# A graph layer on one core: where the adjacency and two pairs of h are turned

## Chip, cores, metric

One Trainium2 chip, one core. The metric is the device time of one execution in microseconds (us), the median of several; lower is better. A profile is one further execution taken by the hardware profiler; its span differs from the timed median by a few us.

TensorE does the matmuls, VectorE and ScalarE the elementwise work. Transfers (DMA) are issued by SyncE, ScalarE and GpSimd, each its own in program order (its queue). A semaphore is a counter that engines wait on; each transfer here has one that tells of its landing. The clock is the share of full speed that the profile's records grant to TensorE; it is 1.00 or one half.

## The reference

```python
h = jnp.maximum(layernorm(x), 0.0)                 # x: (64, 256, 256)
out = x + gnn(h, adj, ...)                         # adj: (64, 256, 256), 0/1

def gnn(x, mask, ...):
    h = relu(bn(conv1d(x^T, conv1_w)))             # 1 tap
    h = bn(conv1d(h, conv2_w, pad=8))              # 17 taps
    x_conv = relu(h + x^T)^T
    s = x @ w_se.T + b_se                          # 3 numbers a node
    A = exp(-dist(s, s)) * mask
    x_nmp = A @ relu(x @ w_msg.T + b_msg)
    # a GRU cell: gates r, z, n from [x_conv, x_nmp] and x
    return (1 - z) * n + z * x
```

All is float32. The 64 graphs are handled in 32 pairs; four pairs are a batch, so there are eight batches, 0 to 7.

## The kernel before

The convolution of 17 taps is done in the frequency domain: VectorE transforms a batch forward, TensorE multiplies 16 bins by filter weights (`products`, two bins a call), VectorE transforms back. Then come the gates of the four pairs, during which the next batch is prepared. The weights are streamed for each batch into nine buffers, three bins ahead of their use:

```python
def load_kind(b, n, kind):
    b, n = b + n // BINS, n % BINS
    if b < NB and (n < BINS - 1 or kind < 2):
        WB[b, n, kind] = work.tile([P, DC, D], FP, name="wb", bufs=9)
        ...
        nc.sync.dma_start(out=WB[b, n, kind], in_=filt[m][:, ...])
```

TensorE needs h with channels on the partitions. A pair's h is either transposed on TensorE (`transpose_h`) or by a DMA transpose of its 16-bit halves, in three steps: turn, sort, join. adj is turned in the same way, kept in DRAM and loaded again when it is needed:

```python
def turn_h(i):
    t = late.tile([P, 2 * MC, W], U16, name="hh").bitcast(FP)
    ...                                   # ScalarE: relu(x * rstd + shift) into hh
    TURNED[i] = late.tile([P, 2 * MC, W], U16, name="halves")
    nc.sync.dma_start_transpose(out=TURNED[i]..., in_=t...)
    load_x(i + 2)

def sort_h(i):
    HH[i] = late.tile([P, 2 * MC, W], U16, name="hh")
    ...                                   # four nc.sync.dma_start, HH <- TURNED

def join_h(i):
    ...                                   # two nc.scalar.copy, HT <- HH

def turn_adj(i):
    HALVES[i] = late.tile([P, 2 * MC, W], U16, name="halves")
    nc.sync.dma_start_transpose(out=HALVES[i], in_=adj[...].bitcast(U16))

def keep_adj(i):
    ADJD[i] = dram.tile([...], U16, name="halves_d", bufs=6)
    for k in range(2 * MC):
        nc.sync.dma_start(out=v[k], in_=HALVES[i][:, k])
```

`halves` has one buffer, shared by turned h and turned adj, and all these transfers and the weights go through SyncE's queue, in program order. The end of a batch (`i`: its first pair, `nxt` = i + 4):

```python
gates(i + 2, 0, wait, ...)                # wait() holds turn_h(nxt + 4)
sort_h(nxt + 4)
turn_adj(nxt);     keep_adj(nxt)
aggregate(i + 3);  finish(i + 1);  load_adj(nxt)
turn_adj(nxt + 1); keep_adj(nxt + 1)
gates(i + 2, 1)
join_adj(nxt)
turn_adj(nxt + 2); keep_adj(nxt + 2)
turn_adj(nxt + 3); keep_adj(nxt + 3)
...                                       # then the next batch's products
```

## Time and profile before

Before: 1912.29 us, the median of 4 runs (1909.44 to 1914.62). From the trace I read two lengths for each batch: "products", from the start of the first to the end of the last matmul that reads `wb`, and "gates", from there to the next batch's first (in batch 7, to TensorE's end).

| batch | 0 | 1 | 2 | 3 | 4 | 5 | 6 | 7 |
|---|---|---|---|---|---|---|---|---|
| products, us | 62.2 | 65.8 | 64.7 | 61.0 | 61.6 | 61.0 | 61.4 | 52.7 |
| gates, us | 168.4 | 164.2 | 164.2 | 164.2 | 164.2 | 164.2 | 164.2 | 153.2 |

Batch 7 has the same products as the others and nothing to prepare behind it. How the profile is read: the page gives each engine's busy time, forty slices of the span and the costliest groups. The waits name the engine and line that waited, what released it, then the total in us, how often, and the longest. The queue in order of time gives start, duration, engine and line of the issue, and what is moved where.

ScalarE waits too:

```profile
ACT adj L423 <- DMA adjh<-halves_d: 77.2, 8, 12.2
...
ACT hT L645 <- DMA hh<-halves: 9.4, 1, 9.4
```

The first is the joining of adj that has just been kept by that chain, the second the joining of the sixth pair's h in batch 0.

### The profile page before, as it was taken

What the parts mean: (1) busy time and instruction counts of PE and PEld (TensorE: products, weight loads), DVE (VectorE), ACT (ScalarE), POOL (GpSimd) and SP (SyncE); (2) the same over time, 40 slices, a digit from 0 to 9 for tenths busy, and PEclk for the clock granted to TensorE, in tenths of its full rate; (3) what the DMA queues carried; (4) which work ended last, traced back from release to release, by engine and by line L of the source; (5) the groups of instructions that cost most, each with busy time, mean ns of one, the idle gap of its engine ahead of it and who ended that gap; (6) DMA issues with size and microseconds to landing.
All of it is one profiled execution on the core that took longest, in us unless ns stands there. A gap on an engine that the chain in (4) does not pass through costs nothing.

```text
span 1915.2 us, 21916 instructions
## 1 busy us (share of the span) xinstructions
PE 1822.1 (95%) x7486; PEld 1133.5 (59%) x7486; DVE 1366.1 (71%) x2591; ACT 731.1 (38%) x1447; POOL 226.1 (12%) x368
## 2 busy tenths in 40 slices
PE   6898999799998999899998999989999899999997
PEld 4686444774557645595446844486455855478453
DVE  5877669496786958688495966959677784979522
ACT  3424542255322643236422554225532364224321
POOL 3210101101011010110111110110011100011000
PEclk9988999899998999999999999999999999999999
DMA  6868335662357433583246633575345833445011
GB/s 189 264 215 212 88 68 121 199 180 56 87 122 225 133 86 75 148 253 84 55 104 181 195 76 67 127 213 164 67 87 121 256 103 70 103 140 147 0 42 36
DMA packets 252896, 247.00 MB, mean 129 GB/s; under 512 B 145410, under 2 KB 179486, under 8 KB 252785
## 3 DMA queue, kind: packets, MB, share of 16 engines
q1 hardware_dynamic: 218741, 183.24, 34.7%
q0 software_dynamic: 31936, 60.48, 13.5%
q10 hardware_dynamic: 2108, 1.89, 0.3%
q8 instruction: 59, 0.97, 0.2%
q14 instruction: 52, 0.43, 0.1%
HBM read 156.54 MB, written 44.30 MB: 105 GB/s over the span
## 4 chain that ended last, share of the span: by engine, by line
PE 69%; DMA 14%; SPq 2%; DVE 2%; ACT 1%; issue 0%; POOLq 0%; POOL 0%; ACTq 0%; DVEq 0%
PE acc L480 59%; PE aux L480 7%; DMA halves<-in_adj_dram 5%; DMA halves_d<-halves 5%; DMA wb<-filt 2%; PE aux L484 2%; SPq L403 1%; PE aux L803 1%; DMA halves<-hh 1%; DMA hh<-halves 1%; ACT hh L622 0%; SPq L636 0%; ACT e L804 0%; DVE Yv L59 0%; DVE T L65 0%
## 5 line engine op out<-in xcount | busy, mean ns | idle before, releaser
L480 PE MATMUL acc<-xnm,w_ih 128*128 128x512 f32 x768 | 353.2, 593 | 0.0
L480 PE MATMUL acc<-hT,w_hh 128*128 128x512 f32 x768 | 350.5, 593 | 0.0
L480 PE MATMUL acc<-Yv,w_ih 128*128 128x512 f32 x768 | 342.7, 596 | 1.1 <-ACT Yv L763 1.1
L480 PEld LDWEIGHTS acc<-Yv,w_ih 128*128 128x128 f32 x768 | 146.0, 191 | 184.3 <-issue 180.8
L480 PEld LDWEIGHTS acc<-xnm,w_ih 128*128 128x128 f32 x768 | 145.0, 190 | 175.7 <-issue 175.5
L480 PEld LDWEIGHTS acc<-hT,w_hh 128*128 128x128 f32 x768 | 144.2, 190 | 164.3 <-issue 155.2
L865 DVE SCALAR_TENSOR_TENSOR gn<-tr,gn 128x512 f32<-128x512 f32 x64 | 44.2, 690 | 211.5 <-ACT tr L863 211.2
L863 ACT ACTIVATE tr<-acc,b_rz 128x512 f32<-128x512 f32 x64 | 44.0, 687 | 326.0 <-PE acc L480 326.0
L480 PE MATMUL acc<-V,wb 128*128 128x128 f32 x1024 | 133.6, 287 | 0.0
L891 POOL DMA_DIRECT2D out_dram<-y x64 | 39.4, 620 | 790.7 <-DVE y L890 789.3
L480 PE MATMUL acc<-U,wb 128*128 128x128 f32 x1024 | 125.3, 277 | 6.8 <-DMA wb<-filt 6.8
L480 PEld LDWEIGHTS acc<-V,wb 128*128 128x128 f32 x1024 | 128.6, 204 | 0.0
L480 PEld LDWEIGHTS acc<-U,wb 128*128 128x128 f32 x1024 | 121.2, 194 | 10.5 <-DMA wb<-filt 7.0
L480 PE MATMUL acc<-hT,w_c 128*128 128x512 f32 x256 | 118.3, 605 | 3.9 <-ACT hT L645 2.0
L59 DVE SCALAR_TENSOR_TENSOR V<-T,V 128x256 f32<-128x256 f32 (+2 forms) x224 | 121.6, 610 | 0.3
L480 PE MATMUL acc<-Sv,wb 128*128 128x128 f32 x512 | 74.5, 292 | 44.2 <-DMA wb<-filt 44.2
L745 DVE TENSOR_TENSOR Yv<-p,acc 128x512 f32<-128x512 f32 x32 | 21.9, 686 | 130.6 <-PE acc L480 95.5
L480 PE MATMUL aux<-e,msg 128*128 128x256 f32 x464 | 104.9, 379 | 0.0
L423 ACT COPY adj<-adjh 128x1024 uint16<-128x1024 uint16 x58 | 73.9, 1345 | 77.2 <-DMA adjh<-halves_d 77.2
L480 PEld LDWEIGHTS aux<-e,msg 128*128 128x128 f32 x464 | 87.3, 190 | 17.5 <-issue 7.2
L480 PEld LDWEIGHTS acc<-Sv,wb 128*128 128x128 f32 x512 | 67.7, 205 | 48.5 <-DMA wb<-filt 45.3
L736 ACT COPY p<-acc 128x512 f32<-128x512 f32 x56 | 32.8, 586 | 160.7 <-PE acc L480 132.2
(153 smaller groups left out, 2772.2 us busy)
## 6 DMA issues: line engine op xcount, KB each, us to landing
wb<-filt SPq DMA_DIRECT2D x376, 256.0 KB
y<-in_x_dram POOLq DMA_DIRECT2D x64, 256.0 KB, 5.6
out_dram<-y POOLq DMA_DIRECT2D x64, 256.0 KB, 5.6
x<-in_x_dram SPq DMA_DIRECT2D x60, 256.0 KB
halves_d<-halves SPq DMA_DIRECT2D x116, 128.0 KB
adjh<-halves_d POOLq DMA_DIRECT2D x116, 128.0 KB, 6.1
hh<-halves SPq DMA_DIRECT2D x112, 128.0 KB
filt<-fo POOLq DMA_DIRECT2D x20, 252.0 KB, 5.6
```

Source lines behind the costliest of these rows:

```text
L59: return self.step(out, lambda: self.v.scalar_tensor_tensor(out, x, s, y, op0=ALU.mult, op1=ALU.add))
L403: nc.sync.dma_start(out=v[k], in_=HALVES[i][:, k])
L423: nc.scalar.copy(v[:, j], u[:, j])
L480: nc.tensor.matmul(p, w, v, **kw)
L484: nc.tensor.transpose(p, v, ident)
L736: nc.scalar.copy(p1, p[0])
L745: nc.vector.tensor_sub(re, pv[0], pv[2])
L803: nc.tensor.matmul(p[:, :N], ZT[rows_q, :P], ZT[rows_q, P:], start=True, stop=True)
L863: nc.scalar.activation(tr, pr, AF.Tanh, bias=b_rz[:, dc:dc + 1], scale=0.5)
L865: nc.vector.scalar_tensor_tensor(gn, tr, 1.0, gn, op0=ALU.add, op1=ALU.mult)
L891: nc.gpsimd.dma_start(out=rows(out, G * i + g), in_=row_tile(Y[i], g))
```

## The change

The intent: spread the turnings of adj over the gates' stretch, one behind each sorting of h, so that one instead of four stands in front of the next batch's weights; and in batch 0, turn the fifth pair's h on TensorE, without the queue, and the sixth pair's h earlier.

```diff
-            if i >= PB:
+            if i > PB:                       # shift is only needed by turn_h
...
-        run(norm_steps(nxt if b == 0 else nxt + 1)[0])
+        if b == 0:
+            norm(nxt)
+        else:
+            run(norm_steps(nxt + 1)[0])
...
         if b == 0:
-            turn_h(nxt)
+            pace.add(norm_steps(nxt + 1)[0], normed[1])
...
             transpose_a(i + 1)
-            sort_h(nxt)
+            transpose_h(nxt)
...
         message(i + 2)
-        if b > 0:
-            turn_h(nxt + 1)
+        pace.flush(normed[1])
+        turn_h(nxt + 1)
 
         def wait():
             pace.flush(scaled)
-            if b == 0:
-                join_h(nxt)
...
         load_adj(i + 3)
-        if b == 0:
-            pace.flush(normed[1])
-            turn_h(nxt + 1)
         sort_h(nxt + 1)
+        turn_adj(nxt)
+        keep_adj(nxt)
...
         sort_h(nxt + 2)
+        turn_adj(nxt + 1)
+        keep_adj(nxt + 1)
...
         sort_h(nxt + 3)
+        turn_adj(nxt + 2)
+        keep_adj(nxt + 2)
...
         sort_h(nxt + 4)
-        turn_adj(nxt)
-        keep_adj(nxt)
+        turn_adj(nxt + 3)
+        keep_adj(nxt + 3)
...                                           # the other three are gone from here
```

More of the change, by code (lines that the diff above doesn't have):

```diff
@@ L1008 @@
         join(0)
-        if b == 0:
-            pace.add(norm_steps(nxt + 1)[0], normed[1])
         pace.add(norm_steps(nxt + 2)[0], normed[2])
@@ L1036 @@
         load_adj(i + 3)
-        if b == 0:
-            pace.flush(normed[1])
-            turn_h(nxt + 1)
         sort_h(nxt + 1)
+        turn_adj(nxt)
+        keep_adj(nxt)
         def early():
@@ L1084 @@
         load_adj(nxt)
-        turn_adj(nxt + 1)
-        keep_adj(nxt + 1)
         gates(i + 2, 1)
         join_adj(nxt)
-        turn_adj(nxt + 2)
-        keep_adj(nxt + 2)
-        turn_adj(nxt + 3)
-        keep_adj(nxt + 3)
         pace.flush(joined[3])
```

## The prediction

> **What bounds the kernel now.** I read the busy table and the slices first, then TensorE's waits, then the DMA queue (SyncE) in order of time, then windows of 20 us.
>
> ```profile
> PE 1822.1 (95%) x7486; PEld 1133.5 (59%) x7486; DVE 1366.1 (71%) x2591; ACT 731.1 (38%) x1447; POOL 226.1 (12%) x368
> ...
> PEclk9988999899998999999999999999999999999999
> ```
> TensorE is busy 95% of the span, VectorE, the next, 71%. So the kernel is bound by TensorE, and only what TensorE waits for, or runs slowly through, can be won. The clock row shows a dip at four slices beyond the start: something stops TensorE there.
>
> TensorE's waits, in total, times, longest:
> ```profile
> PE acc L480 <- DMA wb<-filt: 50.9, 7, 10.2
> ...
> PE acc L480 <- ACT hT L645: 2.0, 1, 2.0
> ```
> Seven waits for `wb`, the filter weights of the products in the frequency domain, are more than half of TensorE's 93 us of idleness. Asked window by window, one (6.8 us) lies at 161 us, inside the first batch's products; the other six (10.2, 9.3, 5.6, 6.6, 5.9, 6.6: 44.2 us) lie just after the start of the products of batches 1 to 6. The boundary into batch 7 has none. Why, is in the queue's own order of time, here into batch 3:
>
> ```profile
> 742.25 2.04 SPq L625 DMA_TRANSPOSE halves<-hh  x1
> 744.34 1.46 SPq L377 DMA_DIRECT2D x<-in_x_dram  x2
> 746.57 2.64 SPq L636 DMA_DIRECT2D hh<-halves  x4
> 752.77 4.83 SPq L394 DMA_TRANSPOSE halves<-in_adj_dram  x1
> 759.67 2.33 SPq L403 DMA_DIRECT2D halves_d<-halves  x4
> 769.11 2.34 SPq L394 DMA_TRANSPOSE halves<-in_adj_dram  x1
> 776.67 2.22 SPq L403 DMA_DIRECT2D halves_d<-halves  x4
> 784.55 2.38 SPq L394 DMA_TRANSPOSE halves<-in_adj_dram  x1
> 789.90 2.23 SPq L403 DMA_DIRECT2D halves_d<-halves  x4
> 797.80 4.21 SPq L394 DMA_TRANSPOSE halves<-in_adj_dram  x1
> 804.00 2.22 SPq L403 DMA_DIRECT2D halves_d<-halves  x4
> 806.27 4.93 SPq L702 DMA_DIRECT2D wb<-filt  x7
> ```
> One turning of h and one sorting, then four times a turning of adj and its keeping in DRAM, each waiting for the one before because all share the single buffer `halves`. Only at 806.27 may the queue issue weights, though the products began at 799.3. Bins 0 to 2 were loaded a batch earlier; bin 3 comes too late. The windows show the price:
>
> ```profile
> 800.00:820.00 20.00, 14.42 (x107) 13.68 (x106) 2.27 (x4) 4.13 (x17) 0.00 (x0) 0.83 0.72 211
> 1700.00:1720.00 20.00, 20.00 (x176) 19.37 (x176) 10.30 (x21) 5.59 (x20) 0.00 (x0) 1.00 0.70 221
> ```
> At the boundary into batch 3 TensorE is busy 14.4 of 20 us at clock 0.83; into batch 7 it is busy throughout at 1.00, and does 176 matmuls instead of 107. The last batch has the same products, so it is my yardstick.
>
> **What the Trainium skill says.** "DMA: Bandwidth & Descriptors", section on the anatomy of one DMA: a wait for a semaphore happens on the issuing sequencer, before dispatch. The trace agrees: the weights, which need nothing of adj, stand behind the keeping's wait. "TensorE: Matmul & The Clock Gate", "Why this matters for your kernels": an idle gap of over about 3 us puts the clock back to half. The trace agrees: at each of the seven waits its clock record goes to one half for 6.8 to 13.7 us, and at full rate for 218 us at a stretch between. "Perfetto Trace Analysis", "Identifying the Most-Contended Engine": matmul busy share is no measure of closeness to roofline; so I work with stage lengths, not with the 95%.
>
> **The change, part by part.**
>
> (1) *adj turned behind each sorting.* No transfer is added or removed; three of four turn-and-keep pairs move out of the tail into the gaps after earlier sortings. From the first to the last matmul that reads `wb`, the products of batches 1 to 7 take 65.8, 64.7, 61.0, 61.6, 61.0, 61.4 and 52.7 us by the trace's starts. If nothing holds up the weights, the six become 52.7: 13.1 + 12.0 + 8.3 + 8.9 + 8.3 + 8.7 = **59.3 us**. Of this 44.2 is the waits, and 15.1 is matmuls at half clock after them. In the tail one adj turning remains: it starts at 752.8, and the next one's start at 769.1 shows it is kept by then, 30 us before the products need the queue.
>
> Does each new place have room? Between the sorting's first issue (746.57) and the start of the second adj turning (769.11), by when `halves` is free again, lie 22.5 us. The gaps from one sorting to the next turning of h, in batch 2, are: 653.1 to 671.7 (18.6 us), 676.1 to 703.8 (27.7), 708.2 to 742.3 (34.1). The first is 4 us short, so the third pair's turning slips 4 us: issued near 675.7, sorted and landed (4.4 + 5.9 us, the durations at 742) near 686. ScalarE joins that pair's halves at 689.1, and TensorE needs the result at 700.9, so the slip is hidden. The second gap then holds the work to within 1 us. The stretch from products' end to the next products takes 164.2 us in every batch 1 to 6, with no wait of TensorE beyond 0.5 us; I leave it there.
>
> (2) *First batch: pair nxt (the fifth) transposed on TensorE.* It removes one turning of h, its sorting, and the joining on ScalarE (2.5 us). The queue stood at 152.5 to 157.6 with that turning and its x load, and from 160.4 for 8.3 us with the sorting, in front of weights: this made the 6.8 us wait. Batch 0's products take 62.2 us. The floor is the yardstick 52.7, plus 1.0 because batch 0 turns two pairs' A (8 transposes, 1.04 us each) where the yardstick has one such group for finish, plus 0.9 for the 8 new transposes: 54.6. But VectorE now also scales x (4 x 0.41 us, from the row of the earlier scalings) behind a wait of some 1.4 us for GpSimd's power, and takes the sixth pair's statistics (1.9 us) here; it is already 98% busy from 140 to 160 us, with some 1.8 us slack before the gates read the first residual. I charge 2.4 us for that and for weights still tight in a window with DMA share 0.98 to 1.03: 57, a gain of **5.2 us**.
>
> (3) *Sixth pair turned ahead of the gates.* Its turning goes from 207 us to just after the keeping of adj 3, about 189. The one wait for `hT` (2.05 us) should go, with part of the half-clock stretch that ran into these gates. Batch 0's gates stretch takes 168.4; floor 164.2 + 0.9 (one more transpose of A) = 165.1; I expect 166, a gain of **2.4 us**.
>
> Sum: 59.3 + 5.2 + 2.4 = 66.9; 1913.15 - 66.9 = 1846.3. Prologue, tail and batch 7 are untouched.
>
> **The rivals.** (a) *A new wait for h.* An adj turning and keeping ahead of each h turning could run longer beside the y and adjh traffic and make ScalarE, then TensorE, wait in `hT`. Against: the slack is 3 us at ScalarE and about 12 at TensorE, the gates' stretches have a DMA share of 0.0 to 0.6, and the turn-and-keep varies only from 12.3 to 18.6 us from start to start. If each of the six batches lost 3 us, the time would be 1864.
> (b) *DMA bandwidth is the bound of the products.* If the weights themselves arrived at TensorE's pace or slower, the wait would shift to later bins. For: share 0.8 to 0.96, some 250 GB/s there. Against: batch 7 streams the same weights in 52.7 us. Half the gain lost: about 1880.
> (c) *VectorE takes over.* It is busy 19.3 to 19.9 of 20 us in late products and in the forward transform. For: it loses its idle 17 us at the boundaries. Against: it is idle there because it has nothing to do, and 16.8 of 20 us just before the boundary says that the forward transform is done in time. With 3 us a batch, 1864.
> (d) *All fits and batch 0 comes down to its floor:* 59.3 + 7.6 + 3.3 = 70.2, so 1843.
>
> **Range and chances.** Centre 1847 (the sum, rounded up, since surprises add time). The lower end 1839 is (d) with 4 us for spread; the upper end 1864 is (a) or (c). Faster by over 2% needs under 1874.9: two fifths of the gain may be lost and it still holds: 0.95. Within 2%: 0.04. Slower: 0.01.
>
> **What would show it right or wrong.** Right: no `wb` wait at any batch boundary, products of 52.7 us in batches 1 to 6, clock 1.00 from batch 0's gates to the last batch, TensorE over 98% busy; the queue in time order shows one turn-and-keep behind each sorting, and weights issued as soon as TensorE frees their buffers; ScalarE's 77.2 us of waiting for `adjh` mostly gone. Step 1 is wrong if TensorE waits for `hT` (room misjudged) or the gates stretch exceeds 164.2. Step 2 is wrong if batch 0's products stay near 62, with `wb` or a VectorE wait. Step 3 is wrong if a wait for `hT` stays near 215 us. The prediction as a whole fails if the waits of the first boundary return a few bins later.

## The result and the profile after

After: 1841.43 us, the median of 4 runs (1840.59 to 1847.17), against 1912.29 us. The ratio is 0.9636, with a 95% interval of 0.9612 to 0.9661: faster. A ratio is the mean time of one kernel's fast runs over that of the other's of the same rounds, so it is not quite the ratio of the medians.

The page after, its busy time and the clock in forty slices:

```profile
PE 1799.6 (98%) x7494; PEld 1113.2 (61%) x7494; DVE 1366.5 (74%) x2594; ACT 729.6 (40%) x1443; POOL 225.1 (12%) x367
...
PEclk9999999999999999999999999999999999999999
```

TensorE's busy time fell by 22.5 us although it does eight matmuls more. 15.9 us of this lie in products 1 to 6 and 2.3 in batch 0, where the clock record no longer goes to one half; 4.2 lie in the start and the last gates, which the change does not touch. TensorE's waits after, as before total, times, longest:

```profile
PE aux L501 <- DMA bn_rows<-in_bn_v_dram: 7.1, 1, 7.1
PE acc L480 <- ACT fo L690: 6.5, 6, 2.3
PE acc L480 <- DMA points<-points: 4.7, 1, 4.7
...
PE acc L480 <- ACT hT L645: 1.0, 1, 1.0
```

No wait for `wb` is left; the three longest are in the start, before the first products. The queue in order of time, batch 2's gates up to batch 3's products:

```profile
613.27 2.66 SPq L636 DMA_DIRECT2D hh<-halves  x4
619.25 2.74 SPq L394 DMA_TRANSPOSE halves<-in_adj_dram  x1
624.10 2.48 SPq L403 DMA_DIRECT2D halves_d<-halves  x4
632.93 1.99 SPq L625 DMA_TRANSPOSE halves<-hh  x1
...
637.23 2.65 SPq L636 DMA_DIRECT2D hh<-halves  x4
643.45 3.19 SPq L394 DMA_TRANSPOSE halves<-in_adj_dram  x1
648.78 2.33 SPq L403 DMA_DIRECT2D halves_d<-halves  x4
664.02 2.03 SPq L625 DMA_TRANSPOSE halves<-hh  x1
...
713.18 4.54 SPq L394 DMA_TRANSPOSE halves<-in_adj_dram  x1
719.86 2.56 SPq L403 DMA_DIRECT2D halves_d<-halves  x4
760.60 3.89 SPq L702 DMA_DIRECT2D wb<-filt  x5
```

One turning and keeping stands behind each sorting. The last keeping is issued at 719.86; the products begin at 759.5, and at 760.60 the first weights are issued, as soon as TensorE frees a buffer. A window of 20 us over that boundary (columns: busy us and count of TensorE, weight loads, VectorE, ScalarE, GpSimd; clock; DMA share; GB/s):

```profile
755.00:775.00 20.00, 20.00 (x159) 18.44 (x158) 9.14 (x18) 6.41 (x21) 1.98 (x4) 1.00 0.77 224
```

TensorE is busy throughout, at full clock. ScalarE's wait for adj fell from 77.2 to 21.5 us:

```profile
ACT adj L423 <- DMA adjh<-halves_d: 21.5, 7, 7.4
```

The lengths by batch ("products 0" are those of batch 0), for this profile and those of all experiments that follow, with the timed medians; "before" is that of the same chip and job:

| kernel | products 0 | gates 0 | products 1 to 6, sum | gates 1 to 6, sum | timed | before | ratio |
|---|---|---|---|---|---|---|---|
| before | 62.2 | 168.4 | 375.5 | 985.2 | 1912.29 | | |
| after | 54.1 | 166.3 | 315.5 | 985.2 | 1841.43 | 1912.29 | 0.9636 |
| r_after | 54.1 | 165.1 | 315.5 | 985.3 | 1845.47 | 1908.62 | 0.9663 |
| r_after2 | 54.1 | 165.1 | 315.5 | 985.2 | 1845.36 | 1908.18 | 0.9676 |
| e_adj_only | 63.0 | 175.8 | 315.5 | 985.3 | 1865.15 | 1908.62 | 0.9767 |
| e_h_only | 54.1 | 165.1 | 369.4 | 985.3 | 1899.97 | 1908.62 | 0.9944 |
| e_wb_act | 59.5 | 169.5 | 367.8 | 985.3 | 1907.51 | 1908.62 | 0.9992 |
| e_wb_pool | 60.3 | 169.1 | 353.4 | 985.3 | 1890.19 | 1912.18 | 0.9883 |
| e_move_one | 54.1 | 165.1 | 315.4 | 985.2 | 1844.16 | 1912.18 | 0.9655 |
| e_fifth_only | 54.1 | 174.5 | 315.5 | 985.2 | 1856.54 | 1912.18 | 0.9716 |
| e_double_first | 54.1 | 178.4 | 315.5 | 993.9 | 1863.32 | 1912.18 | 0.9740 |
| e_wb_pool6 | 63.1 | 167.5 | 327.1 | 985.3 | 1865.76 | 1908.18 | 0.9772 |
| e_points_first | 54.1 | 165.1 | 315.5 | 985.2 | 1842.24 | 1908.18 | 0.9660 |

From before to after the profile gained 60.0 us in products 1 to 6, 8.1 in products 0 and 2.1 in gates 0: 70.2 us, and the timed medians differ by 70.9. The two profiles' spans differ by 76.3 us; the rest is 4.2 us in the start (109.8 against 105.6 us until the first products) and 1.7 us in the last gates. Neither comes from the change: over the profiles of this table, whose start is the same but in e_points_first, it takes 105.6 to 113.5 us, and the last gates take about 153 us in eight profiles and 151.5 in five. The loss of 60.0 us is that of one profile of the kernel before, an execution of 1917 us, 5 us over its median: e_h_only, with the same chain in its tail, lost 53.9, and in the two later jobs with a repeat the timed medians before and after differ by 63.2 and 62.8 us in all.

### The profile page after: what moved, and what is told of

Same layout as the page of the kernel before. It is cut to its first block, busy times and chain, and to the rows that moved or that the text cites. A ratio compares the mean times of both kernels' runs of the same rounds, so it can differ in the third digit from the quotient of the medians.

```text
span 1838.9 us, 21875 instructions
## 1 busy us (share of the span) xinstructions
PE 1799.6 (98%) x7494; PEld 1113.2 (61%) x7494; DVE 1366.5 (74%) x2594; ACT 729.6 (40%) x1443; POOL 225.1 (12%) x367
## 4 chain that ended last, share of the span: by engine, by line
PE 89%; DVE 4%; DMA 4%; issue 1%; ACT 1%; POOL 1%; POOLq 0%; SPq 0%; ACTq 0%; DVEq 0%
PE acc L480 76%; PE aux L480 9%; PE aux L484 2%; PE aux L803 1%; DMA filt<-fo 1%; DMA points<-points 1%; DVE Yv L59 1%; DMA x<-in_x_dram 1%; DVE Yv L62 1%; DVE T L65 1%; DMA halves<-hh 0%; DMA hh<-halves 0%; POOL filt L691 0%; DMA b_msg<-in_msg_b_dram 0%; DVE msg L775 0%
## 5 line engine op out<-in xcount | busy, mean ns | idle before, releaser
L480 PE MATMUL acc<-V,wb 128*128 128x128 f32 x1024 | 124.8, 275 | 0.0
L480 PEld LDWEIGHTS acc<-V,wb 128*128 128x128 f32 x1024 | 119.5, 192 | 0.0
L528 POOL TENSOR_TENSOR rstd<-rstd,neg_half 128x4 f32<-128x4 f32 x32 | 37.4, 1169 | 455.7 <-DVE shift L530 368.1
L870 ACT ACTIVATE nn<-gn,bn_columns 128x512 f32<-128x512 f32 x64 | 46.2, 722 | 115.6 <-DVE gn L868 115.6
L480 PE MATMUL aux<-w_msg,hT 128*128 128x259 f32 x384 | 89.5, 382 | 0.0
L480 PEld LDWEIGHTS acc<-hT,w_c 128*128 128x128 f32 x256 | 48.1, 194 | 62.0 <-issue 52.7
L480 PEld LDWEIGHTS aux<-w_msg,hT 128*128 128x128 f32 x384 | 72.1, 190 | 17.5 <-issue 7.6
```

Of the source, the lines that this page charges most:

```text
L480: nc.tensor.matmul(p, w, v, **kw)
L528: nc.gpsimd.tensor_tensor(t["rstd"], t["rstd"], neg_half, ALU.pow)
L870: nc.scalar.activation(nn, gn, AF.Tanh, bias=b_ih[:, 2 * DC + dc:2 * DC + dc + 1])
```

## The experiments

The theory, A: the weights come late because the chain of adj stands in front of them in SyncE's queue. The rivals: the h part or an altered order on VectorE brings much of the gain (B); the adj transfers slow the weights by taking DMA bandwidth, wherever they are queued (C); the new places for adj are on the edge and only just fit (D). All kernels gave correct results.

### Each part alone

e_adj_only has the adj moves on top of the kernel before; e_h_only has the other hunks only, with all four turnings of adj in the tail.

> Only the adj part of the change: three of four turn-and-keep pairs behind the sortings of h, the first batch's h left as before. Theory A (the weights stand behind the adj chain in the queue): products of batches 1 to 6 fall to 52.6 us each, 60 us in all, batch 0 stays at products 62 and gates 168; about 1852 us. Rival B (a good part of the gain comes from batch 0's own changes to h, or from the altered order on VectorE): under 50 us gained, 1865 or more.

> Only the h part: fifth pair transposed on TensorE, sixth turned ahead of the gates, adj left in the tail. Theory A: the six waits for wb of 5.6 to 10.2 us at the boundaries stay, batch 0's products fall from 62.2 to 54 and its gates from 168.4 to 166.3; a gain of about 10 us, 1902 us. Rival B: a gain of 20 us or more, 1892 or less.

> The changed kernel itself, for comparison on the same chip: 1841 us, ratio 0.963. By both parts' sum (60 + 10 us) it should lie 10 us under the adj part alone and 60 us under the h part alone.

Measured: 1865.15, 1899.97 and 1845.47 us. The adj part alone brings all the 60.0 us of products 1 to 6, to a tenth; the h part alone leaves a loss of 53.9 us there (369.4 against 315.5), of which 40.7 are waits for `wb`:

```profile
PE acc L480 <- DMA wb<-filt: 40.7, 6, 8.5
```

So A holds for products 1 to 6. But e_adj_only missed its time by 13 us, and by that time it lies on B's side (1865 us or more, under 50 us gained); e_h_only lies on A's. The gains, 43.5 and 8.7 us, do not add up to the whole's 63.2: on top of the adj moves the h part is worth 19.7 us, nearly a third, and not the 10 expected. So B, as a statement on the whole gain, is in part right. The difference lies in batch 0. Its products keep their wait for `wb`, and its gates grow: 175.8 us with the adj part alone, against 168.4 before and 165.1 with both (r_after). TensorE's waits of e_adj_only from 160 to 350 us:

```profile
PE acc L480 <- DMA wb<-filt: 7.6, 1, 7.6
PE acc L480 <- ACT hT L645: 6.5, 2, 4.1
```

With the sixth pair still turned late, the turnings of adj behind the next sortings have no room in batch 0, and h itself comes late. The h part is needed to make that room.

### The sixth pair left late

e_fifth_only is the changed kernel, with this undone:

```diff
-        pace.flush(normed[1])
-        turn_h(nxt + 1)
+        if b > 0:
+            turn_h(nxt + 1)
...
         load_adj(i + 3)
+        if b == 0:
+            pace.flush(normed[1])
+            turn_h(nxt + 1)
```

> The changed kernel with the sixth pair turned where it was before, behind the first gates. My sum gave the sixth pair 2.4 us, so 1847 to 1848 us. In the adj part alone batch 0's gates took 175.8 us with two waits for hT: if the late sixth pair is their cause, they stay here (products of batch 0 at 54, gates at 174 or more, some 1855 us); if the fifth pair's turning was their cause, the gates fall to 166 to 168.

Measured: 1856.54 us; products 0 at 54.1, gates 0 at 174.5, with three waits for `hT` between 100 and 350 us:

```profile
PE acc L480 <- ACT hT L645: 5.2, 3, 2.9
```

So the late sixth pair is the cause. Given the adj moves, its earlier turning is worth 8 to 9 us in the profile (174.5 against 165.1 to 166.3) and 12 us in the timed runs of the same job (against e_move_one, which also has two turnings elsewhere), not 2.4. The 8.1 us of products 0 are the fifth pair's alone.

### Order or bandwidth: the first weights from another queue

e_wb_act is the kernel before with

```diff
-            nc.sync.dma_start(out=WB[b, n, kind], in_=...)
+            eng = nc.scalar if b > 0 and n in (3, 4) else nc.sync
+            eng.dma_start(out=WB[b, n, kind], in_=...)
```

> The kernel before with one difference: the weights of bins 3 and 4 of batches 1 to 7 are issued on ScalarE's queue instead of SyncE's. The adj turnings and keepings stay where they were, at the same time and in the same number. Theory A (order in the queue): the six boundary waits vanish, products 53 us in batches 1 to 6, about 1853 us. Rival C (DMA bandwidth: the weights are slow because turnings and keepings take the engines): the waits stay at half their length or more, 1880 us or more.

Measured: 1907.51 us, no gain. That looks like C, but ScalarE's own issues in order of time, here into batch 3, show that the weights were not issued in time:

```profile
788.19 0.33 ACTq L703 DMA_DIRECT2D wb<-filt  x1
789.09 0.33 ACTq L703 DMA_DIRECT2D wb<-filt  x1
789.98 10.64 ACTq L703 DMA_DIRECT2D wb<-filt  x4
800.66 0.58 ACT L737 COPY p<-acc 128x512 f32<-128x512 f32 x1 [10.76 <-DMA halves_d<-halves]
```

Four issues took 10.64 us. In the trace each transfer names its completion semaphore, and in this program the transfers of SyncE and of ScalarE take the same eight in turn; before one is used again, the issuing engine waits for the last transfer that had it. The fourth weight's semaphore was that of the last turning of adj (it got it at 794.65), the fifth's and sixth's those of its keepings (798.85 and 800.24). The chain held the weights from another queue, and ScalarE, waiting, held TensorE by its late copy (TensorE's wait at all six boundaries, 3.7 to 11.3 us, names that copy). So this run tells nothing about C.

GpSimd's transfers use eight other semaphores. e_wb_pool is the same edit with `nc.gpsimd`, and e_wb_pool6 sends bins 3 to 8 there.

> As e_wb_act, but the weights of bins 3 and 4 of batches 1 to 7 are issued on GpSimd's queue. On ScalarE's queue the third to sixth of them were seen to wait for completion semaphores that the adj chain on SyncE's queue still held; GpSimd's transfers use eight others. Theory A2 (the weights wait for their turn: for the queue and for a free completion semaphore, not for bandwidth): boundary waits under 2 us, products of batches 1 to 6 at 53 to 55 us, about 1855 us. Rival C (bandwidth): products stay at 58 us or more although the weights are issued in time, 1885 us or more.

> As e_wb_pool, with bins 3 to 8 instead of 3 and 4 on GpSimd's queue. With two bins, the wait ahead of bin 3 was gone in all six batches, but in four a wait stood ahead of bin 5, the first that came from SyncE again, and the last turning of adj took some 16 us instead of 4 to 7. Theory A2 (order): with six bins issued elsewhere no wait of over 2.5 us is left, products of batches 1 to 6 at 53 to 54 us, 320 us in all, about 1855 us. Rival C (contention of weights and turnings in the DMA engines is a cause of its own): waits stay within bins 3 to 8, products at 55 to 58 us, 1865 to 1885 us.

Measured for e_wb_pool: 1890.19 us; products 1 to 6 are 353.4 us, 22.1 less than before. From the start of one matmul to the next, the gap ahead of bin 3, 5.9 to 10.4 us in all six batches before, is gone in all six; a gap of 3.3 to 7.8 us now stands ahead of bin 5, the first from SyncE again, in four of them (2.0 and 2.4 us in the other two), and one of 5.3 us ahead of bin 4 in batch 2. By its numbers, 1890 us and 58.9 us a batch, this run lies on rival C's side; but the weights of bin 5 were not issued in time, so its condition is not met. SyncE's waits from 540 to 600 us hold

```profile
SPq L403 <- DMA halves<-in_adj_dram: 22.3, 3, 11.9
```

that is, a keeping waited 11.9 us for its turning (longest before: 5.6), while the weights were loading beside it: the last turning was issued at 564.8 and done at 581.1. It is one of six; the last turnings at the other five boundaries took 4.3 to 7.8 us.

Measured for e_wb_pool6: 1865.76 us; products 1 to 6 are 327.1 us. Of the 60.0 us of loss, 48.4 are regained with every adj transfer still in the tail. TensorE's waits for `wb` from 330 to 1700 us, in the kernel before, e_wb_pool and e_wb_pool6:

```profile
PE acc L480 <- DMA wb<-filt: 44.2, 6, 10.2
...
PE acc L480 <- DMA wb<-filt: 26.4, 8, 7.4
...
PE acc L480 <- DMA wb<-filt: 6.2, 6, 2.5
```

So order, in the queue and for the semaphores, is the main cause. No wait of over 2.5 us is left, as A2 said, but the time lies at the near end of C's range (1865 to 1885 us), and the products, 54.5 us a batch, lie between the two. So there is contention too, and the trace shows it: the landings of GpSimd's transfers can be read. The weights of bins 3 and 4, issued 1.3 to 5.8 us after the products' start, landed 3.0 to 4.0 us later in batch 7 of both runs, whose adj chain had ended 30 us before its products; in batches 1 to 6 they took 3.0 to 12.5 us in e_wb_pool and 3.0 to 9.6 in e_wb_pool6. Of the remaining 11.6 us, 5.9 lie in batch 5, where these weights took up to 9.6 us and the turning beside them 12.3. Which of the adj transfers (turning, keeping, loading again) slows the weights is not separated.

### One turning moved is enough

e_move_one is e_h_only with one turning and keeping moved:

```diff
         sort_h(nxt + 1)
+        turn_adj(nxt)
+        keep_adj(nxt)
...
         sort_h(nxt + 4)
-        turn_adj(nxt)
-        keep_adj(nxt)
```

> The h part of the change, and of adj only the first turn-and-keep moved behind a sorting; three stay in the tail. Theory A2 (lateness of the chain's end, some 7 us against the products' first need): a tail shorter by 15 us ends in time, products of batches 1 to 6 at 52.6 us, the same time as the whole change, 1845 us, ratio 0.966. Rival C (the adj traffic in the tail slows the weights by its amount): three quarters of the loss stay, some 1885 us.

Measured: 1844.16 us, ratio 0.9655, with products 1 to 6 at 315.4 us. With three of the four turnings still in the tail nothing is lost. The loss is a matter of lateness: before, SyncE's first weights went out 6.9 to 11.1 us after the products' start at the six boundaries, and a chain one link (13 to 19 us) shorter ends in time. It also means that two of the three moves bring spare time, not time.

### How much room the tightest gap has

e_double_first is the changed kernel with the turning and keeping behind the first sorting done twice (the second writes the same data again).

> The changed kernel with the turning and keeping behind the first sorting done twice: 13.4 us more in the tightest gap, result unchanged. My prediction gave that gap 3 us of slack before ScalarE waits and 12 before TensorE does. If so, ScalarE waits some 7 us for hh in each of seven batches and TensorE loses 0 to 4 us a batch: 1845 to 1873 us. Rival D (the room is much smaller, and the change is on the edge): 8 us a batch or more, over 1900 us.

The queue of this run in batch 2:

```profile
631.08 2.66 SPq L636 DMA_DIRECT2D hh<-halves  x4
637.43 1.97 SPq L394 DMA_TRANSPOSE halves<-in_adj_dram  x1
...
650.60 2.42 SPq L394 DMA_TRANSPOSE halves<-in_adj_dram  x1
...
663.99 1.76 SPq L625 DMA_TRANSPOSE halves<-hh  x1
```

The gap is 32.9 us instead of 19.7. Measured: 1863.32 us. ScalarE waited 51.9 us in 13 waits for `hh`; TensorE lost 8.7 us in the gates of batches 1 to 6 together, 1.4 us a batch, and 12 to 13 us in batch 0. So D falls for batches 1 to 6: with 13 us more in the tightest gap nearly all is still hidden. Batch 0 has less room.

### The start

After the change TensorE's remaining waits over 3 us are in the start. e_points_first issues the small matrices of powers ahead of the taps.

> The changed kernel with the small matrices of powers (points) issued ahead of the taps instead of behind the first third of them: TensorE's longest wait that is left, 4.7 to 8.5 us at 20 us. If the matrices alone were late, the first products start 3 to 7 us sooner: about 1839 us against 1844 of the changed kernel. If the taps land at the same time anyway, no difference (1844). The start of the first products differs by 8 us between runs of unchanged code, so only the timed runs can tell.

> The changed kernel again, for the comparison with the matrices ahead on the same chip: 1841 to 1846 us, ratio 0.963 to 0.967.

Measured: 1842.24 us, ratio 0.9660 (0.9644 to 0.9675), against 1845.36 us, ratio 0.9676 (0.9661 to 0.9690). The wait for `points` is gone, and one for the taps has taken its place:

```profile
PE acc L490 <- DMA taps<-in_c_wT_dram: 5.8, 2, 4.0
```

The medians differ by 3 us and the intervals of the ratios overlap, so no kernel here is shown to beat the changed one.

## Why the prediction was right

The time lies in the range, 5.6 us under the centre; the two repeats on other chips gave 1845.4 and 1845.5. The predicted gain was 66.9 us; the medians of the three jobs give 70.9, 63.2 and 62.8.

- **Step 1**, 59.3 us in products 1 to 6: 60.0 measured, against the same profile of the kernel before (its loss varies, as said under the table). The split was right too: e_h_only shows 40.7 us of waits in a loss of 53.9, the rest matmuls at half clock. The yardstick from batch 7 held to 0.1 us a batch.
- **Its check of room**: the first gap grew from 18.6 to 19.7 us, not by 4, because turning and keeping took less time there (from the sorting's issue to the free buffer 19.7 us, not the 22.5 taken from the tail). No slip reached TensorE: gates 1 to 6 stayed at 985.2 us.
- **Step 2**, 5.2 us in products 0: 8.1 measured, or 5.4 to 9.0: the five profiles that leave batch 0's h as before have 59.5 to 63.1 us. The mis-sized term is the charge of 2.4 us for VectorE and tight weights: products 0 took 54.1 us, even below my floor of 54.6. No wait of TensorE stands there.
- **Step 3**, 2.4 us in gates 0: 2.1 in the first profile after, where a wait for `hT` of 1.0 us is left at 250 us, and 3.3 in the repeats, which have none. As the change's net effect on that stretch the size was right; as the worth of the sixth pair's move it was not. I treated the parts as a sum of independent terms, but the adj moves cost batch 0's gates 7.4 us when alone, and the sixth pair's move takes that back. The sum came out because I had not charged the cost to step 1 either; that was luck.
- **The signs**: no `wb` wait at a boundary, right. Clock 1.00 from batch 0's gates to the last, right: the trace has no half-clock stretch between 100.7 us and 1831.3, when the last matmul has ended. TensorE "over 98%": 1799.6 of 1838.9 is 97.9%, just short. ScalarE's wait for adj "mostly gone": 77.2 to 21.5 us.
- **The rivals**: (a) and (c) did not come about in batches 1 to 6. But (a)'s mechanism is what cost e_adj_only 6.5 us of waits for `hT` in batch 0 (2.0 before), which the prediction had not looked at. Its reading that the gates' stretches have a DMA share of up to 0.6 was too low: it is 0.76 from 1420 to 1440 us. (b), as stated, did not come about either; but the late landings in e_wb_pool and e_wb_pool6 show that adj and weights can slow each other when they run together, which the change avoids by keeping them apart.

## What to carry to other kernels

When the busiest engine waits for a load, look at what stands in front of that load on its queue, and compare how late it is with the length of one link: moving a single link may win everything. Another queue is no way out if its transfers wait for the same completion semaphores. And before work goes into gaps, check the gaps of the first round as well as the steady ones, since parts of a change can make room for each other.

## What the Trainium skill lacked or had wrong

- "DMA: Bandwidth & Descriptors", rules for kernel authors, says that spreading DMAs over the issuing engines does not help bandwidth and only saves sequencer issue time. It leaves out the waits in front of an issue. Here spreading saved 48.4 us of 60.0 in products 1 to 6 when six bins of weights went to GpSimd's queue, because they no longer stood behind waits of other transfers.
- No page that I read says that transfers of two queues can hold each other up through shared completion semaphores. Here four issues on ScalarE's queue took 10.64 us for that reason.
- The same page, under latency and other measured facts, gives DMA transposes 261 GB/s effective, and 350 to 400 when contiguous. A turning of adj, 512 KB, took 4.85 us in the gates (issued at 619.25, its keeping issued at 624.10), some 108 GB/s with its latency. Beside loads of weights from GpSimd's queue two of twelve took 16.4 and 12.3 us, the others 4.3 to 7.8. That is one size of transfer; the page's rate for longer ones is not shown wrong.
- "TensorE: Matmul & The Clock Gate" warns of idle gaps over about 3 us; its section on a second failure mode tells of frequent short idling with the same effect, but gives no lengths. In the last batch's gates two gaps of 0.46 and 1.08 us, next to matmuls of nine rows, were followed by 3.4 us at half clock in eight of thirteen profiles, and by none in five with the same gaps, which is the 1.7 us between 153.2 and 151.5. Why it differs is not shown.
